# Two-layer image kernel: layer norm root as ln and exp on ScalarE, gates of two blocks in one instruction, statistics of the new x in two instructions

## The chip, the cores and the metric

The kernel runs on one core of a Trainium2 chip. The time is that of the device, in microseconds, from launch to end; the kernel before takes 6283.66 us (median of 3 runs, 6276.35 to 6298.06). The core's engines are named as in the profile: PE (TensorE, matmul), PEld (its weight loads), DVE (VectorE), ACT (ScalarE), POOL (GpSimd) and SP (SyncE, which here only issues DMAs).

## The reference

The input x is 4 x 384 x 64 x 64 in f32. Two layers are applied one after the other, each as x + layer(group norm of x) with 32 groups of 12 channels:

```python
x = x + _L0_conv_ref(_gn(x), ...)   # a selective scan over the 4096 tokens of an image
x = x + _L1_conv_ref(_gn(x), ...)   # attention over 3x3 neighbourhoods
```

Only the first layer is changed. What it computes, cut to its core:

```python
xn = (xs - mu) * jax.lax.rsqrt(var + 1e-05) * ln_w + ln_b    # layer norm over 384 channels
xb, z = jnp.split(jnp.einsum('blc,dc->bld', xn, in_proj_w), 2, axis=-1)   # 768 + 768
xc = _silu(conv of 4 taps along l of xb + conv_b)
dt, Bm, Cm = the three parts of xc @ x_proj_w.T               # 24, 16, 16
dt = jax.nn.softplus(dt @ dt_w.T + dt_b)
h = exp(dt_t * A) * h + (dt_t * x_t) * B_t                   # scan over the tokens, 768 x 16 states
y_t = sum over the states of h * C_t
out = ((y + xc * D) * _silu(z)) @ out_proj_w.T
```

The softplus is computed as ln(1 + exp(..)), so the first layer uses exp and ln on ACT everywhere, and a few silus.

## The kernel before

**Tiles.** The four images have 4096 tokens each. They are cut into 17 chunks of 241 tokens (TM), one image after the other, 68 chunks in all. The 384 channels are 3 tiles (NCB) of 128 partitions, three neighbouring channels to a partition, so that a group of 12 channels is 4 partitions; the 768 inner channels are 6 blocks (NJ). The scan of a chunk runs in 12 steps ("units"), two to a block, so a chunk is 12 steps and the layer has 816.

**One step** (the loop over s at the end of `mamba_layer`). POOL and DVE each make half of the scan's input, `h<-dxr,bc` in `s_inputs` and `h<-dxr,bp` in `s_inputs2`; ACT makes the decays `da` by 8 exps (`s_decay`); DVE scans twice (`s_scan`); POOL multiplies the states by C (`s_outputs`, `h<-h,bc`). After every second step PE sums the states into y (`s_sum`, tile y in the PSUM pool `py`, which has one buffer), and DVE multiplies y by the silu of z in place (`s_gate`, `zs<-y,zs`). A block's gate stands at the start of the step after its sum; these are the steps 4, 6, 8, 10 of its chunk and 0 and 2 of the next.

**Order.** Every engine's instructions stay in program order (class `InOrder`; for this reason the profile gives line 45 to all of them, and one goes by tiles). What isn't scan is laid into the steps by a table written by hand: `plan` maps (step, place) to functions, where a chunk's own scan runs from step 24 to 35, and a step has the places EARLY, READY, SCAN, POOL, MID and LATE, in this order:

```python
(-7, EARLY): [f_var],
(-7, MID): [f_root],
(-6, SCAN): [f_pow],
(-5, READY): [f_rs],
```

Modulo 12 these are the steps 5, 6 and 7 of the chunk that is being scanned. In the same steps another chunk's dt is finished: `f_plog` (Ln on ACT into tile ps_lg) and `f_dtx` (DVE product with xc) stand at 5 READY and 5 MID, 6 EARLY and 6 SCAN, 6 SCAN and 7 READY. `ends` holds what ends a chunk: `e_project` (PE, tile ps_out, then an ACT copy into xr) at 4 READY, 6 EARLY and 6 POOL, and `e_store` (statistics of the new x on DVE, store to x1) at 3 EARLY. In `e_project` PE can start as soon as its bank is there.

**Layer norm** of a chunk: `f_var` sums the squares over channels with PE into ps_var, tokens on partitions; `f_root` adds 1e-5 (DVE), `f_pow` raises to -0.5 (POOL), `f_rs` spreads the result over the partitions by PE (ps_rs), `f_scale` applies it (DVE).

**PSUM.** The pool `pmm` has two banks, and ps_ln, ps_var, ps_rs, ps_in, ps_lg, ps_out and the other matmuls of the front, and the norms' sums, take turns in them. The others hold the decays (`pda`), B (`pbb`) and y (`py`).

**Group norm.** `x_coeffs` (first layer) and `e_store` (for the second) collect bn_stats, and `group_norm_coeffs` joins them: bn_aggr for each of the 3 tiles, then sums over the 4 partitions of a group by matmuls with the matrix blk12, first of the means, then of variances and squared deviations.

Of the kernel before, what the change touches and what calls it, by code (L numbers as in the profile page):

```python
# [7 lines left out]
F32 = mybir.dt.float32  # L8
# [4 lines left out]
P = 128  # L13
# [7 lines left out]
TM = 241  # L21
# [25 lines left out]
        return call  # L47


def group_norm_coeffs(pe, ve, ae, gp, small, psum, blk12, mhalf, st, sc, bi):  # L50

    mv = small.tile([P, NCB, 2], F32, tag="mv", name="mv")
    neg = small.tile([P, 1], F32, tag="mg", name="neg")
    dev = small.tile([P, NCB], F32, tag="dev", name="dev")
    for cb in range(NCB):
        ve.bn_aggr(mv[:, cb, :], st[cb])
    yield False
    ps = psum.tile([P, 2, TM], F32, tag="mm", name="pm")  # L60
    for cb in range(NCB):
        pe.matmul(ps[:, 0, 0:1], blk12, mv[:, cb, 0:1], start=(cb == 0), stop=(cb == NCB - 1))
    yield True
    ae.mul(neg, ps[:, 0, 0:1], -1.0)
    ae.activation(dev, mv[:, :, 0], AF.Square, bias=neg)
    yield False
    ps = psum.tile([P, 2, TM], F32, tag="mm", name="pv")
    for cb in range(NCB):
        pe.matmul(ps[:, 0, 0:1], blk12, mv[:, cb, 1:2], start=(cb == 0), stop=False)
    for cb in range(NCB):  # L70
        pe.matmul(ps[:, 0, 0:1], blk12, dev[:, cb : cb + 1], start=False, stop=(cb == NCB - 1))
    yield True
    ve.tensor_scalar_add(sc, ps[:, 0, 0:1], 1e-5)
    gp.tensor_tensor(sc, sc, mhalf[:, 0:1], ALU.pow)
    yield False
    ae.mul(bi, neg, sc)
# [3 lines left out]
def mamba_layer(ctx, tc, x, w, x1, sc1, bi1, consts, behind):  # L80
# [13 lines left out]

    nc = tc.nc
    B, _, L = x.shape
    blk12, ident, eps, one = consts
    pe, ve, ae, gp, sp = (
        InOrder(tc, e) for e in (nc.tensor, nc.vector, nc.scalar, nc.gpsimd, nc.sync)
    )  # L100
# [46 lines left out]
    def x_coeffs(b):  # L147


        st = [xstats[b][:, cb].rearrange("p a s -> p (a s)") for cb in range(NCB)]  # L150
        sc = small.tile([P, 1], F32, tag="sc0", name="sc0")
        bi = small.tile([P, 1], F32, tag="bi0", name="bi0")
        avs = small.tile([P, P], F32, tag="avs", name="avs")
        bc = small.tile([P, 1], F32, tag="bc0", name="bc0")

        def parts():
            yield from group_norm_coeffs(pe, ve, ae, gp, small, pmm, blk12, mhalf, st, sc, bi)
            ae.mul(avs, avg, sc)
            yield False
            pb = pmm.tile([P, 2, TM], F32, tag="mm", name="pb")  # L160
            pe.matmul(pb[:, 0, 0:1], avg, bi, start=True, stop=True)
            yield True
            ve.scalar_tensor_tensor(bc, pb[:, 0, 0:1], -float(NCB), bi, ALU.mult, ALU.add)

        norms.append([parts(), False])
        coeffs[b] = (sc, avs, bc)
# [125 lines left out]
    def f_root(c):  # L292
        n = c.spans[0][1]
        c.vs = front.tile([P, 2], F32, tag="vs", name="vs")
        ve.tensor_scalar_add(c.vs[:n, :], c.pv[:n, :, 0], 1e-5)

    def f_pow(c):
        n = c.spans[0][1]
        gp.tensor_tensor(c.vs[:n, :], c.vs[:n, :], mhalf[:n, :], ALU.pow)

    def f_rs(c):
        c.ps = pmm.tile([P, 2, TM], F32, tag="mm", name="ps_rs")
# [168 lines left out]
    def at(f, *args):  # L471
# [9 lines left out]
        (-10, READY): [f_center],  # L481
        (-9, POOL): [f_square],
        (-7, EARLY): [f_var],
        (-7, MID): [f_root],
        (-6, SCAN): [f_pow],
        (-5, READY): [f_rs],
        (-5, SCAN): [f_scale],
# [159 lines left out]
    def s_sum(u, u2):  # L647

        c, t = u.c, u.t
        y = py.tile([P, TM], F32, tag="y", name="y")  # L650
        pe.matmul(y[:, :t], ddiag[:, u.j, :], c.xc[:, u.j, :TM], start=True, stop=False, skip_group_check=True)
        for g in range(NG):
            for i in range(4):
                h4 = (u, u2)[i // 2].h4
                pe.matmul(
                    y[CG * i : CG * (i + 1), :t],
                    ssum,
                    h4[:, i % 2, g, :TM],
                    start=False,
                    stop=(g == NG - 1),  # L660
                    skip_group_check=True,
                )
        u2.y = y

    def s_gate(u):
        c, t = u.c, u.t
        ve.tensor_mul(c.zs[:, u.j, :t], u.y[:, :t], c.zs[:, u.j, :t])


    st1 = {}  # L670
# [17 lines left out]

    def e_store(c):
        if c.ci == 0:  # L690
            st1[c.b] = small.tile([P, NCB, NC, 6], F32, tag="st1", name="st1")
        for cb in range(NCB):
            ve.bn_stats(st1[c.b][:, cb, c.ci, :], c.xr[:, cb, c.lo : TM])
        sp.dma_start(e_tokens(c, x1), c.xr[:, :, c.lo : TM])
        if c.ci == NC - 1:
            b = c.b
            st = [st1[b][:, cb].rearrange("p a s -> p (a s)") for cb in range(NCB)]
            made = group_norm_coeffs(
                pe, ve, ae, gp, small, pmm, blk12, mhalf, st, sc1[:, b : b + 1], bi1[:, b : b + 1]
            )  # L700
            norms.append([made, False])

# [73 lines left out]
    for s in range(-4, NU * (len(chunks) + 2)):  # L776
        k, m = divmod(s, NU)
        if m % 2 == 0 and unit(s + 4) is not None:
            s_fetch(s + 4)
        parts(s, EARLY)  # L780
        if m % 4 == 3 or s >= NU * len(chunks):
            norm_part(False)

        if (u := unit(s + 1)) is not None:
            s_inputs2(u)
        if (u := unit(s - 3)) is not None and not u.first:
            s_gate(u)
        parts(s, READY)

        b, ci = chunks[k][:2] if 0 <= k < len(chunks) else (B, 0)  # L790
        if b + 1 < B:
            n, e = divmod(NU * ci + m - 3, NU // 2)
            if e == 0 and 0 < n <= NCB * NX:
                x_stat(b + 1, n - 1, pending.pop())
            if e == 1 and 0 <= n < NCB * NX:
                pending.append(x_load(b + 1, n))
            if e == 2 and n == NCB * NX:
                x_coeffs(b + 1)
        for i in range(2):
            if (u := unit(s)) is not None:  # L800
                s_scan(u, i)
            if i == 1:
                parts(s, SCAN)
            if (u := unit(s + 1)) is not None:
                if i == 0:
                    s_carry(u)
                s_decay(u, i)
            if i == 0 and (u := unit(s - 1)) is not None:
                s_save(u)
        if (u := unit(s - 1)) is not None:  # L810
            s_outputs(u)
        norm_part(True)
        parts(s, POOL)
        if (u := unit(s + 2)) is not None:
            s_inputs(u)
        if (u := unit(s - 2)) is not None and not u.first:
            s_sum(unit(s - 3), u)
        parts(s, MID)
        parts(s, LATE)
        if s == front_end:  # L820
            fronts.close()
        if s >= front_end:
            over = das[0] if s >= NU * len(chunks) - 1 else None
            behind(lambda: pmm.tile([P, 2, TM], F32, tag="mm", name="psv").rearrange("p a b -> p (a b)"), over)
# [385 lines left out]
@with_exitstack  # L1210
def layers(ctx, tc, w, out):
    nc = tc.nc
    x = w["x"]
    B, _, H, W = x.shape
    dram = ctx.enter_context(tc.tile_pool(name="dram", bufs=1, space=bass.MemoryType.DRAM))
    cp = ctx.enter_context(tc.tile_pool(name="cp", bufs=1))
    x1 = dram.tile([B, C, H * W], F32, tag="x1", name="x1")
    blk12 = cp.tile([P, P], F32, tag="blk12", name="blk12")
    nc.sync.dma_start(blk12, w["blk12"])
    ident = cp.tile([P, P], F32, tag="ident", name="ident")  # L1220
    nc.sync.dma_start(ident, w["ident"])
    eps = cp.tile([P, 1], F32, tag="eps", name="eps")
    nc.gpsimd.memset(eps, 1e-5)
    one = cp.tile([P, 1], F32, tag="one", name="one")
    nc.gpsimd.memset(one, 1.0)
    sc1 = cp.tile([P, B], F32, tag="sc1", name="sc1")
    bi1 = cp.tile([P, B], F32, tag="bi1", name="bi1")
    consts = (blk12, ident, eps, one)
    weights, ready = {}, []
    later = outlook_before(ctx, tc, w, x1, H, W, sc1, bi1, dram, weights, ready)  # L1230

    def behind(*room):
        try:
            later.send(room if started else None)
        except StopIteration:
            pass
        started.append(True)

    started = []
    mamba_layer(tc, x.rearrange("b c h w -> b c (h w)"), w, x1, sc1, bi1, consts, behind)  # L1240
    outlook_layer(tc, x1, w, out, sc1, bi1, weights, ready)


def layouts(inputs):
# [34 lines left out]
    f = np.float32  # L1279
    a["ident"] = np.eye(P, dtype=f)  # L1280
    a["avg"] = np.full((P, P), 1.0 / C, f)
    a["blk12"] = np.kron(np.eye(P // 4, dtype=f), np.full((4, 4), 1.0 / 12.0, f)).astype(f)
    a["onesc"] = np.full((P, 1), 1.0 / C, f)
    r = np.arange(P)
    k = np.arange(2 * NS)
# [22 lines left out]
```

## Time and profile before

| | of the profiled execution |
|---|---|
| time shown for it | its span, 6278.2 us from the first to the last instruction; the three runs 6276.35 to 6298.06, median 6283.66 |
| mean granted PE clock | 0.934 |
| first layer's scan steps | about 150 to 5046 us of the span, 71.36 us for a quiet chunk |
| DVE scans `h<-da,h` | x1632, 2158 ns each |
| ACT decay exps `da<-dtr,aneg` | x6528, 465 ns |
| POOL `h<-h,bc`, `h<-dxr,bc` | x816 each, 3953 and 1990 ns |
| DVE `h<-dxr,bp` | x816, 1142 ns |
| PE `y<-h,ssum` | x13056, 406 ns |
| DVE gates `zs<-y,zs` | x408, 404 ns |
| DVE `st<-xr` (statistics of the new x) | x192 of 241 elements, 400 ns, and x12 of 240 |
| DVE `vs<-ps_var` and POOL `vs<-vs,mhalf` | x68 each, 136 and 699 ns |

A row of the groups reads: engine, operation, output<-inputs, shape, how often, then total busy us and mean ns of one, then the idle time of the engine just ahead and what ended it. A mean counts an instruction from its start to its end; on a queue two neighbours overlap a little, so the distance between starts is shorter. A row of the timeline reads: start, duration, engine, operation, tiles, and in brackets how long the engine had been idle and what released it. A row of waits: who waited for whom, total us, times, longest. Of the profiled execution only the span is shown, and no device time of its own.

### The profile page before, as it was taken

How to read it: one execution, taken by the hardware profiler on the slowest of the kernel's cores; microseconds unless marked ns; L12 is line 12 of the kernel's file. 1: busy time of each engine (PE TensorE's matmuls, PEld its weight loads, DVE VectorE, ACT ScalarE, POOL GpSimd, SP SyncE). 2: the span in 40 equal slices, each digit the busy share in tenths (PEclk: the TensorE clock that was granted, in tenths of full speed). 3: DMA queues.
4: the chain of work that ended last, by engine and by line, in shares of the span. 5: the costliest groups of instructions: out<-in, count | busy, mean ns of one | idle time of the engine just before them, and what ended most of it. 6: DMA issues, size and time to landing. Idle time of an engine off the chain costs nothing. (4 is left out here: it accounts for less than half of the span.)

```text
span 6278.2 us, 113454 instructions
## 1 busy us (share of the span) xinstructions
PE 5607.8 (89%) x40506; PEld 3965.2 (63%) x40506; DVE 5371.6 (86%) x4786; ACT 4990.9 (79%) x11842; POOL 5308.6 (85%) x2047
## 2 busy tenths in 40 slices
PE   6888988888888889988888888899888789999999
PEld 5666666666666666666666666666666455555555
DVE  4999999999999999999999999999999954445444
ACT  3888898888888888989888889888898845444544
POOL 3999999999999999999999999999999944433333
PEclk9999999899999999999999999999999899999999
DMA  4555555545555645555555545455545644454554
GB/s 128 133 134 147 146 135 133 133 129 143 147 138 132 146 129 138 146 132 136 141 137 147 140 126 136 129 134 139 135 125 135 167 149 162 165 170 165 173 169 146
DMA packets 640843, 894.22 MB, mean 142 GB/s; under 512 B 130249, under 2 KB 535163, under 8 KB 640148
## 3 DMA queue, kind: packets, MB, share of 16 engines
q1 hardware_dynamic: 640276, 886.96, 51.8%
q8 instruction: 319, 5.23, 0.4%
q14 instruction: 248, 2.03, 0.1%
HBM read 660.89 MB, written 225.70 MB: 141 GB/s over the span
## 5 line engine op out<-in xcount | busy, mean ns | idle before, releaser
L45 DVE TENSOR_TENSOR_SCAN h<-da,h 128x968 f32<-128x968 f32 x1632 | 3452.5, 2158 | 83.4 <-issue 48.5
L45 ACT ACTIVATE da<-dtr,aneg 128x241 f32<-128x241 f32 x6528 | 3036.8, 465 | 296.1 <-DVE h L45 133.5
L45 POOL TENSOR_TENSOR h<-h,bc 128x1928 f32<-128x1928 f32 x816 | 3225.4, 3953 | 12.7 <-DVE h L45 8.0
L45 POOL TENSOR_TENSOR h<-dxr,bc 128x964 f32<-128x964 f32 x816 | 1623.6, 1990 | 116.4 <-PE y L45 95.3
L45 PE MATMUL ps_in<-u,win 128*128 128x241 f32 x4896 | 1078.8, 374 | 83.4 <-DVE dtx L45 75.9
L45 PEld LDWEIGHTS ps_in<-u,win 128*128 128x128 f32 x4896 | 911.9, 191 | 248.2 <-DVE dtx L45 100.1
L45 POOL TENSOR_TENSOR bd<-ain,own 99x1188 f32<-99x1188 f32 x192 | 413.4, 2181 | 726.5 <-DMA ain<-ad 550.6
L45 DVE TENSOR_TENSOR h<-dxr,bp 128x964 f32<-128x964 f32 x816 | 931.6, 1142 | 109.2 <-PE y L45 93.8
L45 PE MATMUL y<-h,ssum 128*32 128x241 f32 x13056 | 907.2, 406 | 28.6 <-POOL h L45 27.7
L45 PEld LDWEIGHTS y<-h,ssum 128*32 128x32 f32 x13056 | 434.7, 119 | 442.8 <-issue 213.2
L45 PE MATMUL ps_cv<-xb,cdiag 128*128 128x241 f32 x3264 | 694.2, 368 | 5.7 <-ACT neg L45 4.7
L45 PEld LDWEIGHTS ps_cv<-xb,cdiag 128*128 128x128 f32 x3264 | 611.4, 189 | 78.5 <-issue 13.5
L45 PE MATMUL psv<-wv,xp 128*128 128x384 f32 x1728 | 592.8, 495 | 7.2 <-issue 7.2
L45 PE MATMUL ps_xd<-xc,wx 128*56 128x241 f32 x816 | 307.9, 559 | 323.1 <-ACT xc L45 323.1
L45 ACT ACTIVATE bd<-ain,own 99x324 f32<-99x324 f32 x704 | 334.6, 556 | 264.6 <-PE ps L45 240.6
L45 PE MATMUL ps_out<-zs,wout 128*128 128x241 f32 (+1 forms) x2448 | 537.2, 369 | 0.0
L45 DVE TENSOR_TENSOR fold<-fold,ps 128x192 f32<-128x192 f32 (+1 forms) x768 | 211.3, 303 | 333.2 <-PE ps L45 318.8
L45 PEld LDWEIGHTS ps_out<-zs,wout 128*128 128x128 f32 x2448 | 470.5, 192 | 36.5
L45 PEld LDWEIGHTS psv<-wv,xp 128*128 128x128 f32 x1728 | 322.7, 191 | 232.3 <-issue 18.1
L45 PEld LDWEIGHTS ps_xd<-xc,wx 128*56 128x56 f32 x816 | 154.6, 199 | 464.1 <-ACT xc L45 348.5
L45 ACT COPY vst<-psv 128x384 f32<-128x384 f32 x279 | 130.8, 470 | 322.3 <-PE psv L45 322.3
L45 PE MATMUL ps_dt<-xd,wdt 25*128 25x241 f32 x816 | 253.0, 436 | 113.5 <-ACT dt L45 80.4
(108 smaller groups left out, 5503.2 us busy)
## 6 DMA issues: line engine op xcount, KB each, us to landing
dxr<-dxd SPq DMA_DIRECT2D x1632, 120.5 KB
dtr<-dtd SPq DMA_DIRECT2D x1632, 120.5 KB
bc<-bcd SPq DMA_DIRECT2D x544, 120.5 KB
vin<-vd SPq DMA_DIRECT2D x384, 148.5 KB
vd<-vst SPq DMA_DIRECT2D x93, 576.0 KB
dxd<-dtx SPq DMA_DIRECT2D x272, 180.8 KB
dtd<-dt SPq DMA_DIRECT2D x272, 180.8 KB
xs<-in_x SPq DMA_DIRECT2D x96, 256.0 KB
```

The source lines that it names most:

```text
L45: return self.tc.keep_in_program_order(issue(*args, **kwargs))
```

## The change

Four edits, all in the first layer and the norms:

- **Root.** `f_root` becomes an ACT Ln with bias 1e-5, at LATE of step -7 instead of MID; `f_pow` becomes an ACT Exp with scale -0.5, in its place. DVE's add and POOL's pow of the chunks are gone (those in `group_norm_coeffs` stay).
- **Gates.** The y of two blocks lies in one tile of 2 x 241, and one DVE instruction gates both, after the odd block: at the steps 6, 10 and 2 instead of six times.
- **Statistics of the new x.** bn_stats over two channel tiles at once (482 elements) and over the third, instead of three.
- **Group norm.** As each partition now aggregates all its elements at once, there is one bn_aggr, one matmul for the mean and two for the variance, with the matrix blk4 of 1/4 for blk12 of 1/12.

```diff
@@ group_norm_coeffs
-    for cb in range(NCB):
-        ve.bn_aggr(mv[:, cb, :], st[cb])
+    ve.bn_aggr(mv, st)
...
-    for cb in range(NCB):
-        pe.matmul(ps[:, 0, 0:1], blk12, mv[:, cb, 0:1], start=(cb == 0), stop=(cb == NCB - 1))
+    pe.matmul(ps[:, 0, 0:1], blk4, mv[:, 0:1], start=True, stop=True)
...
-    for cb in range(NCB):
-        pe.matmul(ps[:, 0, 0:1], blk12, mv[:, cb, 1:2], start=(cb == 0), stop=False)
-    for cb in range(NCB):
-        pe.matmul(ps[:, 0, 0:1], blk12, dev[:, cb : cb + 1], start=False, stop=(cb == NCB - 1))
+    pe.matmul(ps[:, 0, 0:1], blk4, mv[:, 1:2], start=True, stop=False)
+    pe.matmul(ps[:, 0, 0:1], blk4, dev, start=False, stop=True)
@@ f_root, f_pow, plan
-        ve.tensor_scalar_add(c.vs[:n, :], c.pv[:n, :, 0], 1e-5)
+        ae.activation(c.vs[:n, :], c.pv[:n, :, 0], AF.Ln, bias=eps[:n, :])
...
-        gp.tensor_tensor(c.vs[:n, :], c.vs[:n, :], mhalf[:n, :], ALU.pow)
+        ae.activation(c.vs[:n, :], c.vs[:n, :], AF.Exp, scale=-0.5)
...
-        (-7, MID): [f_root],
+        (-7, LATE): [f_root],
@@ s_sum, s_gate
-        y = py.tile([P, TM], F32, tag="y", name="y")
+        if u.j % 2 == 0:
+            c.y = py.tile([P, 2, TM], F32, tag="y", name="y")
+        y = c.y[:, u.j % 2]
...
-        u2.y = y
...
-        ve.tensor_mul(c.zs[:, u.j, :t], u.y[:, :t], c.zs[:, u.j, :t])
+        zs = c.zs[:, u.j - 1 : u.j + 1, :t]
+        ve.tensor_mul(zs, c.y[:, :, :t], zs)
@@ e_store
-            st1[c.b] = small.tile([P, NCB, NC, 6], F32, tag="st1", name="st1")
-        for cb in range(NCB):
-            ve.bn_stats(st1[c.b][:, cb, c.ci, :], c.xr[:, cb, c.lo : TM])
+            st1[c.b] = small.tile([P, 2, NC, 6], F32, tag="st1", name="st1")
+        for i, cbs in enumerate((slice(0, 2), slice(2, NCB))):
+            ve.bn_stats(st1[c.b][:, i, c.ci, :], c.xr[:, cbs, c.lo : TM])
@@ the loop over the steps
-        if (u := unit(s - 3)) is not None and not u.first:
+        if (u := unit(s - 3)) is not None and not u.first and u.j % 2:
             s_gate(u)
```

## The prediction

> **What bounds the kernel now.** First I read the page's busy line, to see whether any engine is full:
>
> ```profile
> PE 5607.8 (89%) x40506; PEld 3965.2 (63%) x40506; DVE 5371.6 (86%) x4786; ACT 4990.9 (79%) x11842; POOL 5308.6 (85%) x2047
> ```
>
> Four engines lie between 79 and 89%. The change touches the first layer, about 150 to 5046 us of the span; between 2000 and 3000 us busy time per 1000 us is DVE 969, POOL 982, PE 881, ACT 893. None is full, so a loop over several engines must set the period, and the view of waits names its links:
>
> ```profile
> POOL h L45 <- PE y L45: 95.3, 88, 8.1
> DVE h L45 <- PE y L45: 93.8, 111, 6.2
> ```
>
> (us in total, times, longest.) DVE and POOL start the scan inputs `h<-dxr` and both wait for PE's y, more than once a chunk (68 chunks). I then followed one quiet chunk on the timeline; its period is 71.36 us, and the mean over chunks about 72.1. The loop starts where ACT's decay exps wait for a DVE scan to free `da`:
>
> ```profile
> 2014.83 1.96 ACT L45 ACTIVATE da<-dtr,aneg 128x241 f32<-128x241 f32 x4 [0.65 <-DVE h L45]
> ```
>
> From here ACT runs on without a gap to the dt exps (2041.65, 2044.01), PE does ps_dt and the y of step 5, and DVE's input product follows at 2047.36: 32.53 us. In that stretch DVE isn't binding; in every chunk this product starts 0.50 us (PE at full clock) or 0.86 us (half) after y's last weight load. Step 5 to 6 goes on so (start, duration, then engine and tiles):
>
> ```profile
> 2046.67 0.14 DVE L45 TENSOR_SCALAR vs<-ps_var 121x2 f32<-121x2 f32 x1
> 2046.72 0.65 DVE L45 TENSOR_TENSOR dtx<-ps_lg,xc 128x482 f32<-128x482 f32 x1
> ...
> 2047.36 1.16 DVE L45 TENSOR_TENSOR h<-dxr,bp 128x964 f32<-128x964 f32 x1
> 2047.42 0.30 PEld L45 LDWEIGHTS ps_out<-xr,ident 128*128 128x128 f32 x2 [0.94 <-DVE dtx L45]
> ...
> 2049.15 0.65 ACT L45 ACTIVATE ps_lg<-dt,one 128x482 f32<-128x482 f32 x1
> ...
> 2050.58 0.36 ACT L45 COPY xr<-ps_out 128x241 f32<-128x241 f32 x1 [0.78 <-PE ps_out L45]
> ...
> 2054.51 0.65 DVE L45 TENSOR_TENSOR dtx<-ps_lg,xc 128x482 f32<-128x482 f32 x1
> ...
> 2055.22 1.49 PE L45 MATMUL ps_in<-u,win 128*128 128x241 f32 x6 [1.10 <-DVE dtx L45]
> ```
>
> What to see: ps_out starts 0.06 us after dtx started its last work, waiting for the PSUM bank that dtx gives up; ACT waits 0.78 us for ps_out; the third dtx (2054.51) frees the bank for ps_in; behind ps_in PE does ps_rs and the y of step 7; and DVE's next product (2060.59) has waited 0.42 us for that y. That is 13.23 us. The last 25.61 us, to the next chunk's trigger, are DVE's own scans, products and gates. 32.53 + 13.23 + 25.61 = 71.37.
>
> [...] 137 table loads, which is 1 + 2 x 68, though four Ln and Exp kinds alternate; I add none. [...] 32 y matmuls take 3.44 us at 2043.88 and 1.84 us at 2058.72.
>
> **The change part by part.** The rows concerned (count, total, mean ns, idle before):
>
> ```profile
> L45 DVE TENSOR_TENSOR zs<-y,zs 128x241 f32<-128x241 f32 x408 | 164.9, 404 | 12.4 <-PE y L45 8.5 <-ACT zs L45 3.9
> ...
> L45 POOL TENSOR_TENSOR vs<-vs,mhalf 121x2 f32<-121x2 f32 x68 | 47.6, 699 | 39.9 <-DVE vs L45 39.9
> ...
> L45 DVE TENSOR_SCALAR vs<-ps_var 121x2 f32<-121x2 f32 x68 | 9.2, 136 | 18.3 <-PE ps_var L45 18.3
> ...
> L45 ACT ACTIVATE dev<-mv,neg 128x3 f32<-128x3 f32 x8 | 2.4, 296 | 0.3
> ```
>
> *Gates.* Six single gates a chunk (steps 0, 2, 4, 6, 8, 10) become three of 482 elements (2, 6, 10). On the queue a single one occupies 0.32 us (2061.67 to the scan at 2061.99); for 482 elements I take the f32 product dtx, 2054.51 to 2055.08, 0.57 us. ([...] the trace has 404 and 646.) DVE saves 6 x 0.32 - 3 x 0.57 = 0.21 us a chunk; where they lie decides. Step 4 gone: -0.32 ahead of 2047.36, where y binds, worth 0. Step 2, +0.25: inside 0.77 us that DVE is idle at 2031.04, 0. Step 6, +0.25: in the middle stretch, counted below. Steps 8 and 0 gone, step 10 +0.25: all in the DVE stretch, -0.39 x 68 = **-26.5 us**. The gates' y tiles still go into one buffer, and the pair waits where the odd block's gate waited, so no wait is added.
>
> *Statistics.* bn_stats 3 x 400 ns becomes 693 (the 512-element row) + 400, about -0.1 us on DVE at step 3, ahead of 2047.36: 0, hidden by the same wait for y. The norms lose small aggregates and six matmuls each, partly exposed: -1 us for all.
>
> *Pow off POOL.* 0.65 us of POOL's queue per chunk, 44 us in all. POOL waits 95.3 us for y already and starts the step with y's arrival (2060.73); what it saves turns into more waiting: 0. Without that cover it would be the full 44.
>
> *The DVE add*, 0.05 us of queue: 0, y again. The Exp (at step 6, behind one da group): 0.1 us overlapped, by the 0.296 us of dev.
>
> *Ln on ACT, and the bank.* This is the part with a price. ps_var, ps_lg, ps_out, ps_in and ps_rs share two PSUM banks. Their requests are served in code order, and of two free banks the one whose release was written earlier goes first. Before, ps_var's bank (A) is freed by the DVE add and, just behind, ps_lg's bank (B) by the first dtx. So the second ps_lg gets A, ps_out gets B and starts at once, at 2047.43. After, the root is written at LATE, behind that dtx: B is now freed first and goes to ps_lg, ps_out gets A and must wait for Ln. Ln stands on ACT behind the step's da group, so it runs 2049.15 to about 2049.45 (dev's 0.30), and ps_out starts at about 2049.48 instead of 2047.43: **+2.05**. Queued behind it: on PE the next ps_out and ps_in; on ACT the copy xr, 2050.58 to about 2052.63, behind it (0.07 + the da group 1.96 + st 0.19 + Exp 0.1) Ln of ps_lg, then the third dtx: 3.12 after the copy, so 2055.75 instead of 2054.51. ps_in, ps_rs and y follow dtx, so the middle stretch grows by 1.24; the step-6 pair is hidden behind this. The rest of the 2.05 is ACT's slack (0.53 before ps_lg, and dtx's).
>
> I did this sum for each chunk that the trace shows, 64 of them. In some 24 quiet chunks it gives 1.2 to 1.3; where ps_out was already late by 1 us it gives 0.4 to 0.9, and where y is so late that dtx waits anyway only the pair's 0.25. Mean 0.72; x 68 = **+48.9 us**.
>
> *PE's clock.* PE now idles from y's end (about 2047.3) to 2049.5. [...] The trace of before has no such gap here. Bounds: 0 and 1.9 in all of about 26 quiet chunks, 49 us; I take +6, three or four chunks[...].
>
> *Prologue.* The third chunk's Ln stands ahead of the first ps_lg on ACT and waits for PE: +1 us. The end of the layer waits for a DMA (5.17 us): 0.
>
> Sum: -26.5 + 48.9 + 6 + 1 - 1 = +28.4. On the profiled span, 6278.2, 6306.6. The median shown, 6283.66, is 5.5 above that span, so **6312 us**.
>
> **Rivals.**
> 1. *The banks do not swap*, or ps_out's wait costs nothing. Speaks for it: the allocation is inferred from starts and releases, not shown by a row. Then -26.5 + 0.25 x 68 = -9.5, so 6274: no measurable change. Against: ps_out starts exactly with a dtx release, chunk after chunk.
> 2. *Faster: y of step 5 does not bind.* Its lead over DVE in quiet chunks is only about 0.09 us. If it comes 0.5 us earlier, as from ACT's side it might, DVE's savings ahead of it count too: 0.51 x 68 = 35 us, 6249. It decides as soon as y is early by more than what DVE saves, and no bank is late. Against: 111 waits of DVE for y, and ACT gets no work taken off.
> 3. *The clock falls in all quiet chunks*: +49 instead of +6, 6355[...].
> 4. *POOL is what binds*: -44, 6240. Against: its 95.3 us of waiting.
>
> **How the numbers follow.** Chances: forecast 0.60, own range 6296 to 6335, its median 6312; rival 1 0.21; rivals 2 and 4 together 0.12; rival 3 0.07. A difference under 0.3% (18.9 us: 6264.8 to 6302.5) can't be told from none here. Of the forecast 0.07 lies below 6302.5; rival 1 gives 0.18 same and 0.03 faster; 2 and 4 give 0.10 faster and 0.02 same; rival 3 is slower. Faster 0.13, same 0.27, slower 0.60. The range 6255 to 6345 leaves out most of rivals 2 and 4 and of rival 3, under 0.2.
>
> **What would show it.** Right: ps_out of step 6 with a wait for ACT's vs of about 2 us, starting right behind it, in place of the 0.94 for dtx; the quiet period near 72.2; a single-gate row gone and one of 482 elements x 204 near 646 ns; POOL's wait for y up by about 40 us; table loads still 137. Wrong: ps_out still starting with dtx, or the product at 2047.36 no longer following y by 0.50 us (0.86), or more table loads: 2 x 1.28 us a chunk would be 174 us.

## The result, and the profile after

The changed kernel takes 6369.18 us (median of 4 runs, 6363.45 to 6374.55) against 6280.01 us before (4 runs): ratio 1.0141, 95% interval 1.0123 to 1.0159. It is slower, as forecast, but by 89 us where the sum had 28, and above the top of the range (6345). The profiled execution's span grew from 6278.2 to 6370.7 us, its mean granted clock fell from 0.934 to 0.922.

The page's busy line of the changed kernel (it answers to the first line shown of before):

```profile
PE 5678.6 (89%) x40410; PEld 4002.1 (63%) x40410; DVE 5352.5 (84%) x4430; ACT 5002.1 (79%) x11978; POOL 5265.4 (83%) x1979
```

DVE and POOL have less to do, by 19 and 43 us, ACT hardly more; PE has fewer matmuls and is busy for 71 us longer. Work that takes longer without being more is the first hint. The view of waits (who waited for whom, us in total, times, longest):

```profile
ACT xr L45 <- PE ps_out L45: 251.0, 71, 4.6
...
POOL h L45 <- PE y L45: 223.4, 91, 10.6
DVE h L45 <- PE y L45: 138.4, 136, 7.2
PEld ps_out L45 <- ACT vs L45: 137.2, 64, 3.0
...
PE ps_out L45 <- ACT vs L45: 91.7, 64, 2.2
```

The wait of ps_out for ACT's vs is new, 64 times: the two banks have changed owners as foretold. Behind it, ACT's wait for ps_out went from 100.0 to 251.0 us, POOL's for y from 95.3 to 223.4, DVE's from 93.8 to 138.4. A quiet chunk of the changed kernel on the timeline (quiet: unit 3 to unit 7, from input product to input product, takes about 25.4 us, so y of step 5 is not late); unit 7's input product starts at 681.13, where the chunk shown of before has 2047.36:

```profile
682.89 0.24 ACT L45 ACTIVATE vs<-ps_var,eps 121x2 f32<-121x2 f32 x1
683.04 0.66 ACT L45 ACTIVATE ps_lg<-dt,one 128x482 f32<-128x482 f32 x1
683.19 0.30 PEld L45 LDWEIGHTS ps_out<-xr,ident 128*128 128x128 f32 x2 [2.91 <-ACT vs L45]
683.19 0.68 PE L45 MATMUL ps_out<-xr,ident 128*128 128x241 f32 x2 [2.11 <-ACT vs L45]
...
683.70 4.29 PE L45 MATMUL ps_out<-zs,wout 128*128 128x241 f32 x12
...
688.03 0.36 ACT L45 COPY xr<-ps_out 128x241 f32<-128x241 f32 x1 [4.33 <-PE ps_out L45]
...
691.16 0.66 DVE L45 TENSOR_TENSOR dtx<-ps_lg,xc 128x482 f32<-128x482 f32 x1 [2.54 <-ACT ps_lg L45]
```

ps_out starts 2.06 us behind the product, right behind the Ln, as worked out. But its twelve matmul records (the six f32 matmuls of the kernel leave two each) then take 4.29 us; in the chunk shown of before they took 2.61:

```profile
2047.94 2.61 PE L45 MATMUL ps_out<-zs,wout 128*128 128x241 f32 x12
```

So the copy xr comes 6.90 us behind the product instead of 3.22, and the third dtx 10.03 us behind it instead of 7.15. The windows view says why (columns: stretch, its length, busy us of PE, PEld, DVE, ACT, POOL, then the granted clock and DMA):

```profile
680.90:684.30 3.40, 1.29 (x9) 1.06 (x6) 3.17 (x3) 2.70 (x8) 3.40 (x3) 1.00 0.95 206
684.30:687.70 3.40, 3.40 (x10) 2.65 (x8) 3.40 (x4) 0.00 (x0) 3.40 (x2) 0.51 0.15 44
```

In the first window PE is busy for 1.29 of 3.40 us, since it waits for the Ln; in the next one it is busy throughout, at half clock (0.51 granted).

By stage (distances between the input products of a chunk's units, mean of 64 chunks): unit 7 to unit 9, the middle stretch, went from 13.34 to 14.90 us; unit 3 to unit 7 from 26.27 to 26.51; the rest of the chunk from 32.62 to 32.26. The last is the gates' saving on DVE, -0.36 us.

### The profile page after: what moved, and what is told of

The parts are those of the page before. It is cut to its first block, busy times and chain, and to the rows that moved or that the text cites. A ratio compares the mean times of both kernels' runs of the same rounds, so it can differ in the third digit from the quotient of the medians.

```text
span 6370.7 us, 113038 instructions
## 1 busy us (share of the span) xinstructions
PE 5678.6 (89%) x40410; PEld 4002.1 (63%) x40410; DVE 5352.5 (84%) x4430; ACT 5002.1 (79%) x11978; POOL 5265.4 (83%) x1979
## 3 DMA queue, kind: packets, MB, share of 16 engines
q14 instruction: 247, 2.02, 0.1%
## 4 chain that ended last, share of the span: by engine, by line
ACT 37%; PE 32%; DVE 17%; issue 5%; DMA 2%; SPq 2%; POOL 1%; ACTq 0%; DVEq 0%; POOLq 0%
ACT da L45 25%; DVE h L45 15%; PE psv L45 9%; PE pso L45 4%; PE ps_out L45 4%; PE ps L45 3%; PE ps_in L45 3%; PE y L45 3%; PE psa L45 2%; ACT dt L45 2%; ACT xc L45 2%; ACT L45 2%; SPq L45 2%; PE ps_xd L45 2%; DMA dxr<-dxd 2%
## 5 line engine op out<-in xcount | busy, mean ns | idle before, releaser
L45 POOL TENSOR_TENSOR h<-dxr,bc 128x964 f32<-128x964 f32 x816 | 1622.9, 1989 | 298.2 <-PE y L45 223.4
L45 DVE TENSOR_TENSOR h<-dxr,bp 128x964 f32<-128x964 f32 x816 | 929.3, 1139 | 152.3 <-PE y L45 138.4
L45 PE MATMUL y<-h,ssum 128*32 128x241 f32 x13056 | 922.9, 409 | 34.3 <-POOL h L45 31.2
L45 PE MATMUL ps_out<-zs,wout 128*128 128x241 f32 (+1 forms) x2448 | 594.6, 397 | 0.0
L45 PEld LDWEIGHTS ps_out<-zs,wout 128*128 128x128 f32 x2448 | 512.7, 209 | 51.6
```

Of the source, the lines that this page charges most:

```text
L45: return self.tc.keep_in_program_order(issue(*args, **kwargs))
```

## The experiments

**First group: is it the bank?** One line of the changed kernel is moved:

```diff
-        (-7, LATE): [f_root],
+        (-7, READY): [f_root],
```

> The changed kernel with one line moved: the Ln on ACT at READY of step 5 (just ahead of the first ps_lg) instead of LATE, so that ps_var's bank is given back before the first dtx gives back its own. Bank theory: the first ps_out of step 6 starts again with the end of that dtx (within 0.2 us of the input product, not 1 to 2 us behind it), its matmuls run at full clock, the stretch from the product of unit 7 to that of unit 9 falls from 14.90 us (mean) to 13.3 to 13.7, and the time to 6265 to 6300 us, a ratio of 0.997 to 1.003 to the kernel before. Rival, that ACT's extra work (Ln and Exp, 0.44 us a chunk) or the gate pairs are the price: the time stays within 15 us of the changed kernel's 6369.

Measured: 6279.48 us, ratio 0.9997 (0.9988 to 1.0006). Waits of this kernel:

```profile
POOL h L45 <- PE y L45: 148.3, 103, 9.1
DVE h L45 <- PE y L45: 129.2, 135, 5.8
...
PEld ps_out L45 <- DVE dtx L45: 14.7, 20, 2.0
```

No wait of ps_out for vs is among the waits any more; it waits for dtx again. The middle stretch is 13.66 us. The whole loss is gone though Ln and Exp are still on ACT (244 and 199 ns in the changed kernel), the gates still in pairs. So the price lay in where the Ln stands, not in its work.

The root put back to DVE and POOL, everything else as changed:

```diff
-        ae.activation(c.vs[:n, :], c.pv[:n, :, 0], AF.Ln, bias=eps[:n, :])
+        ve.tensor_scalar_add(c.vs[:n, :], c.pv[:n, :, 0], 1e-5)
...
-        ae.activation(c.vs[:n, :], c.vs[:n, :], AF.Exp, scale=-0.5)
+        gp.tensor_tensor(c.vs[:n, :], c.vs[:n, :], mhalf[:n, :], ALU.pow)
...
-        (-7, LATE): [f_root],
+        (-7, MID): [f_root],
```

> The changed kernel with the root put back as it was (DVE add at MID, POOL pow): gates in pairs, statistics in two instructions, short group norm only. Bank theory: no late ps_out, so the time is that of the kernel before plus -0.39 us (DVE stretch) and +0.25 us (step 6) a chunk, together -9 us: 6255 to 6290, ratio 0.996 to 1.001. Rival, that the pairs cost more than the singles (a later gate, a longer hold of the y tile): above 6300, ratio over 1.003.

Measured: 6284.14 us, ratio 1.0003 (0.9995 to 1.0011). The gates and the statistics are worth nothing by themselves, neither way. By stage they bring -0.33 us in the rest of the chunk and +0.25 in the middle stretch, much as the prediction had them, but also +0.20 from unit 3 to unit 7, where it had nothing. DVE's wait for y rose from 93.8 to 125.5 us: what DVE saves it waits.

The root alone, on the kernel before:

```diff
-        ve.tensor_scalar_add(c.vs[:n, :], c.pv[:n, :, 0], 1e-5)
+        ae.activation(c.vs[:n, :], c.pv[:n, :, 0], AF.Ln, bias=eps[:n, :])
...
-        gp.tensor_tensor(c.vs[:n, :], c.vs[:n, :], mhalf[:n, :], ALU.pow)
+        ae.activation(c.vs[:n, :], c.vs[:n, :], AF.Exp, scale=-0.5)
...
-        (-7, MID): [f_root],
+        (-7, LATE): [f_root],
```

> The kernel before with only the root changed (Ln and Exp on ACT, Ln at LATE), gates and statistics as before. Bank theory: the whole loss and a little more, since the gain of the gates is missing: 6365 to 6395 us, ratio 1.013 to 1.018, ps_out of step 6 waiting for vs in 60 or more chunks. Rival, that the loss comes of root and gates together (the pair at step 6 sits in the late stretch): 6300 to 6340.

Measured: 6381.61 us, ratio 1.0164 (1.0150 to 1.0178); ps_out waits for vs 64 times, 143.1 us on the weight loads. The root alone makes the whole loss and a little more.

The add moved to LATE on DVE, the same turn of the banks with a quick release:

```diff
-        (-7, MID): [f_root],
+        (-7, LATE): [f_root],
```

> The kernel before with one line moved: the root's add stays on DVE and the pow on POOL, but the add is at LATE, behind the first dtx instead of ahead of it. The two banks change owners just as in the changed kernel, but ps_out now waits for a DVE add that follows the dtx at once. If the swap costs only what the releasing instruction is late: ps_out starts about 0.1 us later than in the kernel before, no loss, ratio 0.998 to 1.003. If another turn of the banks costs by itself (who follows on which bank in steps 6 to 8): the stretch from unit 7 to unit 9 grows by over 0.5 us and the ratio is over 1.005.

Measured: 6279.67 us, ratio 1.0001 (0.9992 to 1.0011), middle stretch 13.40 us; ps_out now waits for DVE's vs (34 times) and starts on average 0.01 us later than in the kernel before. Banks that change owners cost nothing here; what costs is the Ln that gives the bank back, queued on ACT behind a group of decay exps (in the quiet chunk shown of the changed kernel four of them, 1.95 us from 681.01).

**Second group: where the other 60 us come from.** Filling matmuls on PE, with constants as operands and a result that nobody reads; the layer's own results are not changed by them. First in the gap of the root-only kernel:

```diff
+    def f_fill(c, count):
...
+        for _ in range(count):
+            pe.matmul(
+                spare["y"],
+                ident,
+                wout.rearrange("p j c q -> p (j c q)")[:, :TM],
...
-        (-7, LATE): [f_root],
+        (-7, LATE): [f_root, at(f_fill, 4)],
```

> The root-only kernel (Ln at LATE) plus four matmuls of 128x128 by 241 on constants, put on PE behind the y of step 5, ahead of the late ps_out; their result goes to an unused half of y's PSUM bank and is read by nobody. Four take about 1.5 us at full clock, so they lie inside the 2.1 us gap of the quiet chunks (and 0.5 us over the 1.0 us gap of the others). Clock theory (the gap lets PE's clock fall, and this is what the sum left out): in the quiet chunks ps_out starts at +2.06 us as in the root-only kernel, but its matmuls run at full clock; unit 7 to unit 9 takes 14.2 to 14.8 us there instead of 16.18, and the time falls from 6382 to 6325 to 6360 us. Rival, that the half clock has nothing to do with the gap: 16.2 us in quiet chunks and a time of 6375 to 6410.

Measured: 6356.41 us, ratio 1.0115 (1.0094 to 1.0137), against 1.0164 without the matmuls. A quiet chunk of it (unit 7 starts at 753.47):

```profile
755.54 0.67 PE L45 MATMUL ps_out<-xr,ident 128*128 128x241 f32 x2 [0.28 <-ACT vs L45]
...
756.05 2.61 PE L45 MATMUL ps_out<-zs,wout 128*128 128x241 f32 x12
758.70 0.36 ACT L45 COPY xr<-ps_out 128x241 f32<-128x241 f32 x1 [2.65 <-PE ps_out L45]
```

The four matmuls take 1.90 us. ps_out starts as late as without them (+2.07 us), but runs its 2.61 us, and the middle stretch of quiet chunks takes 14.5 us instead of 16.2. In 63 of the 64 chunks ps_out now runs at full clock from start to end, without the matmuls in 27. More work on PE made the kernel some 25 us faster: the gap, by way of the clock, is a cause of its own. The gain is a lower bound, since in chunks with the shorter gap the matmuls come on top (ps_out 1.6 to 2.4 us late there instead of about 1.0 to 1.8), and DVE's gate waits for y's bank that they write to (0.67 us in the chunk shown).

Then lateness without a gap, on the kernel before:

```diff
+        (-7, LATE): [at(f_fill, 5)],
```

> The kernel before, root and gates as they were, plus five such matmuls on PE behind the y of step 5, so that ps_out of step 6 starts about 1.9 us late in every chunk, with PE busy in that time and with no work added to ACT. This prices the lateness without a gap. Prediction's sum (late ps_out, late third dtx, late y): unit 7 to unit 9 takes 14.1 to 14.6 us in all chunks instead of 13.34, no ps_out at half clock, time 6330 to 6360, ratio 1.008 to 1.013. Rival, that lateness alone makes the whole loss: 16 us and a ratio of 1.02 or more; rival, that it is the gap alone: ratio under 1.003.

Measured: 6359.62 us, ratio 1.0123 (1.0102 to 1.0144). But DVE's gate waited 94.7 us for y's bank, so lateness and gate are mixed, and the run decides nothing alone. The same five matmuls in ps_out's own bank:

```diff
@@ e_project
+        if cb == 1:
+            for _ in range(5):
+                pe.matmul(
+                    po[:, 1], ident, wout.rearrange("p j c q -> p (j c q)")[:, :TM], start=True, stop=True,
```

> As the kernel before with five idle matmuls ahead of ps_out, but written into the unused half of ps_out's own bank, so that no gate on DVE waits for them (in the last such run DVE's gate waited 94.7 us for y's bank, which the matmuls used). ps_out proper starts about 1.9 us late in every chunk, PE is busy, ACT has no work added. The prediction's sum for lateness alone (late by 1.9 less 0.81 of slack, about +1.0 us a chunk): unit 7 to unit 9 takes 14.0 to 14.5 us, i2 of unit 8 not later than in the kernel before (6.12 us behind unit 7), time 6325 to 6355, ratio 1.008 to 1.012. If most of the last run's loss came of the waiting gate instead: ratio under 1.005.

Measured: 6354.55 us, ratio 1.0115 (1.0102 to 1.0128); unit 8's product at 6.12 us, no gate waiting. Quiet chunks, with ps_out 2.1 to 2.2 us behind the product, take 14.3 to 14.4 us in the middle stretch, where the prediction's sum for 2.12 us behind it has 13.24 + 1.24 = 14.48. So the sum for lateness at full clock holds to within 0.2 us. Lateness costs more in this run than in the changed kernel because ps_out is 2.0 to 2.8 us late in nearly every chunk here, and only 1.0 to 1.7 us in 45 of 64 there.

**Third group: the clock at the y of step 5.** In the kernel before, this y already ran at half clock, in whole or in part, in 63 of 64 chunks. Four such matmuls in the steps ahead of it:

```diff
-        (16, SCAN): [at(f_dt, 1)],
-        (17, EARLY): [at(f_dt, 2)],
+        (16, SCAN): [at(f_fill, 3), at(f_dt, 1)],
+        (17, EARLY): [at(f_fill, 1), at(f_dt, 2)],
```

> The kernel before plus four such matmuls a chunk where PE waits for ACT in steps 4 and 5: three ahead of the second ps_dt, one ahead of the third. In the kernel before, the y of step 5 runs partly at half clock in every chunk, and unit 3 to unit 7 takes 25.4 us in quiet chunks and 26.5 to 28 in the others. If light work and short waits on PE are what lowers the clock there: more chunks at 25.4, the mean of this stretch down from 26.27 to 25.4 to 25.9, and the time down by 25 to 60 us (6220 to 6255, ratio 0.990 to 0.996). If the matmuls get in the way of ps_dt, or the clock doesn't follow them: ratio 1.000 to 1.006.

Measured: 6262.37 us, ratio 0.9967 (0.9957 to 0.9978): faster, at the weak end of the expectation; unit 3 to unit 7 takes 26.02 us, and y runs at full clock throughout in 18 of the 64 chunks. With the Ln at READY and the rest of the change:

> All parts of the change with the Ln at READY (as in the first experiment) plus the same four matmuls in steps 4 and 5. If y then comes early, the gates' savings on DVE ahead of it begin to count: faster than the one before by another 5 to 20 us (6200 to 6245, ratio 0.987 to 0.995). If y's clock isn't what binds: 1.000 to 1.006 as for the first experiment or a little over.

Measured: 6248.86 us, ratio 0.9946 (0.9929 to 0.9962), faster than both kernels. In the chunks where y runs at full clock (22 here, 18 in the run before) unit 3 to unit 7 takes 24.94 us here and 25.32 us there, and the chunk 70.78 against 71.29 us (medians): once y comes early, the gates' savings count.

Ten such matmuls in PE's wait ahead of ps_xd (323.1 us in 67 waits of the kernel before, 4.8 us each), on that kernel:

```diff
-        (14, POOL): [f_bc],
+        (14, POOL): [at(f_fill, 10), f_bc],
```

> The kernel before with ten such matmuls (about 3.7 us) inside PE's 5 us wait for the silus ahead of ps_xd, and none in steps 4 and 5. The clock falls to half right behind this wait and falls again 17.07 us (five windows) later, at the y of step 5, for the same number of windows. If the second fall follows from the first: both go, unit 3 to unit 7 at 25.3 to 25.6 us in most chunks, ratio 0.990 to 0.996. If the second is made by the light work of steps 4 and 5 alone: the first goes, the second stays, ratio 0.998 to 1.002.

Measured: 6299.62 us, ratio 1.0028 (1.0018 to 1.0039), though the mean clock rose from 0.934 to 0.953. The half clock behind the wait, which every one of the 64 chunks had, is left in one; the one at y has stayed in 61 (63 before; there it comes 17.07 us behind the first in 49 chunks and 13.65 us in 14). But in the chunk looked at the matmuls first waited 1.53 us for a DVE gate and then took 4.33 us, and ps_xd starts right behind them, 5.77 us behind unit 3's product against 4.94 in the chunk shown of before; so they also hold ps_xd up. The second fall doesn't follow from the first; the size of this run is not clean. Both fills together:

> All parts of the change with the Ln at READY, the four matmuls in steps 4 and 5 and the ten ahead of ps_xd. If the gap ahead of ps_xd matters for y's clock: better than the 0.9946 of the run without them, 0.985 to 0.993, most chunks near 70.8 us. If not: 0.993 to 0.997.

Measured: 6242.24 us, ratio 0.9936 (0.9923 to 0.9948), not told apart from 0.9946, at a clock of 0.971 against 0.946.

## Why the prediction was wrong

**The part that held.** The bank (ps_out waits for vs 64 times with the Ln at LATE and 34 times with DVE's add at LATE, for dtx with the Ln at READY), the waiting instruction, the start of ps_out to 0.06 us (2.06 behind the product for 2.12), the DVE stretch (-0.36 us a chunk for -0.39), POOL's saving turned into waiting (with the Ln at READY, its wait for y rises by 53 us for about 40), no further table load (137 before and after), the pair's duration (652 ns for 646).

**The step that failed is the term "PE's clock"**: "+6, three or four chunks". Of the 64 chunks read:

| chunks of the changed kernel | number | unit 7 to 9 | over 13.34 | sum |
|---|---|---|---|---|
| ps_out 2.1 us late, then falls to half clock | 18 | 16.24 us | +2.90 | 52 us |
| ps_out 1.0 to 1.2 us late, at half clock from its start | 18 | 15.36 us | +2.02 | 36 us |
| ps_out 1 to 1.7 us late, full clock | 27 | 13.72 us | +0.38 | 10 us |
| the last one read, ps_out at half clock before and after | 1 | 14.38 us | +1.04 | 1 us |

Together 100 us, where the prediction had 0.72 x 64 = 46 for lateness and 6 for the clock. Taking 14.5 us (the run with the filled gap) as the price of a quiet chunk without the fall, 18 x 1.74 = 31 us of it are the fall in the first row. In the second row, ps_out 1 us late at full clock takes 13.55 us; at half clock it is 15.36, so 18 x 1.81 = 33 us. Clock together 64 us, lateness 36 (with the gate pair's 0.25 us a chunk in it, as in the 46). The rival that the prediction gave 0.07, the clock in all quiet chunks, was the case, in 18 chunks where it counted about 26; its 1.9 us for one of them was the author's estimate, and 1.74 was measured. And the second row is something that neither named.

The second row comes of the gap too. Its y ran at half clock, as in 16 such chunks of the kernel before. There PE went from y to ps_out without a pause, and the clock was full again by 1.6 us behind the product, so that ps_out's twelve records took 2.61 to 2.97 us. In the changed kernel PE waits 1.0 to 1.2 us for the Ln, the half clock goes on for another 3.41 us, and they take 3.82 to 4.07. One such chunk before (unit 7's product at 1830.74) and one after (1863.85), at the same place in the windows:

```profile
1828.85:1832.26 3.41, 3.41 (x24) 2.02 (x17) 1.52 (x3) 3.10 (x8) 1.66 (x2) 0.50 0.96 222
1832.26:1835.67 3.41, 2.96 (x14) 2.43 (x14) 3.41 (x2) 1.06 (x4) 3.41 (x3) 1.00 0.01 3
```

```profile
1861.93:1865.34 3.41, 2.38 (x21) 1.08 (x14) 1.49 (x2) 3.28 (x9) 2.09 (x2) 0.50 0.98 227
1865.34:1868.75 3.41, 3.41 (x10) 2.82 (x10) 3.41 (x3) 0.01 (x1) 3.41 (x2) 0.50 0.01 4
```

With the gap filled no chunk is of this kind. The prediction had priced these chunks at 0.25 to 0.9 us, without another window at half clock.

What led it astray: "three or four chunks" was the author's estimate, and no row of before showed what a gap of 2.1 us does to the clock. What the trace of before did show is the slow y at 2043.88, with PE busy for 3.04 of 3.40 us in the window right ahead of it (lines at the end): half clock came there behind a window with no more than 0.36 us of waiting.

**A smaller step**, "Step 4 gone ... worth 0" and "Step 2 ... 0": unit 3 to unit 7 grew by 0.24 us (16 us in all). It does so in both other kernels with pairs and no filling matmuls (26.39 and 26.47) and not with the root alone (26.25); the kernels with single gates and nothing filled in that stretch lie between 26.08 and 26.27, one profiled execution each. So it belongs to the pairs or the statistics: DVE gets there 0.36 us earlier and y does not. What holds y back in that stretch, ACT's chain, POOL's or the clock's windows, was not separated; that it is y is shown by the run in which it comes early.

The sum with measured terms: -0.36 + 0.24 + 1.56 = +1.44 us a chunk, x 67 = 96 us, against 92.5 on the spans.

## What to carry to other kernels

When an instruction gives a shared buffer back, ask behind what it is queued and who gets that buffer next: moving it past one other release can hand the late buffer to the engine that cannot wait (here PE, 64 waits, 91.7 us). Price a delay less the slack in its way; but look at the clock of the work behind a new wait on PE as well: here waits of 2.10 to 2.15 us cost 1.74 us a chunk in this way, in all 18 chunks that had them, and waits of 1.0 to 1.2 us cost 1.81 us in the 18 where they fell into a window at half clock. Look for slow matmuls ahead of a wait that binds before saving work on the engine that does the waiting.

## What the runs showed of the hardware

A gap of 2.10 to 2.15 us was enough to halve PE's clock for the next 3.41 us, in all 18 chunks of the changed kernel with such a gap; PE was busy for 1.26 to 1.31 us of the window that the gap lay in. The windows are those of the trace's clock records, which in the first layer last 3.413 us or a multiple of it.

What a shorter gap did depended on the window that it fell into. In 23 chunks of the changed kernel a gap of 1.0 to 1.7 us lay in a window at full clock, PE was busy for 1.72 to 2.39 us of it, and the clock stayed full. In 18 a gap of 1.0 to 1.2 us lay in a window at half clock, PE was busy for 2.19 to 2.39 us of it, and the half clock went on. A chunk of the first kind, with the same gap of 1.03 us and the same 2.38 us as the one at 1861.93 above:

```profile
2462.68:2466.09 3.41, 2.38 (x15) 2.14 (x12) 3.28 (x3) 1.60 (x4) 3.14 (x2) 1.00 0.39 93
2466.09:2469.50 3.41, 2.96 (x15) 2.43 (x14) 3.41 (x4) 2.44 (x9) 3.41 (x2) 1.00 0.00 0
```

Between the two kinds the clock differs and the work too: the full-clock window holds ps_out's full matmuls, the other mostly y's with 32 columns. Which of them decides was not separated, nor where between these figures the clock turns.

Nor need PE wait that long. Two windows of the kernel before, columns as above:

```profile
2040.50:2043.90 3.40, 3.04 (x22) 2.30 (x22) 3.40 (x3) 3.24 (x9) 3.40 (x3) 1.00 0.97 250
2043.90:2047.30 3.40, 3.40 (x33) 1.36 (x32) 3.40 (x4) 3.27 (x10) 3.40 (x2) 0.50 1.02 260
```

In the first PE is busy for 3.04 us and the next still runs at half clock. Most of its matmuls are thin, ps_dt with 25 rows and ps_var with one column; full ones laid between them took the half clock away from the y that follows in 18 of 64 chunks (a ratio of 0.9967). Whether the thin matmuls or the short waits between them bring the half clock was not tested by itself. And a higher mean clock was no gain in itself: 0.953 went with 1.0028, 0.971 and 0.946 with the same time.
